# Attention steps placed by hand in a two-layer graph transformer kernel, its pairs of tiles, its query bias and the PSUM places of its border queries

## The chip, the core and the metric

The kernel runs on one core of a Trainium2 chip. The metric is device time in microseconds (us) for one execution; the time given for the kernel before is the median of its runs. Five engines work side by side, each on its own instructions in order: PE (matrix multiplication), DVE (vector work), ACT (activations, scaling and copies), POOL (here above all the indirect transfers, called gathers) and SP (which only issues transfers). An instruction waits until what it needs is there, and everything behind it on the same engine waits with it. 16 DMA engines move data between the core's memory and HBM.

## The reference

2708 nodes with 512 features pass through two equal layers of a graph transformer: attention with 8 heads of 64 over the neighbours in an adjacency matrix, then a feed-forward network with 2048 hidden units, each with a residual and a normalization.

```
mask = adj + eye
q, k, v = (h @ Wq.T + bq), (h @ Wk.T + bk), (h @ Wv.T + bv)      # 8 heads of 64
scores = where(mask == 0, -1e9, q . k / 8)
ctx = softmax(scores) @ v
h1 = layer_norm(h + ctx @ Wo.T + bo)
h2 = layer_norm(h1 + relu(h1 @ W1.T + b1) @ W2.T + b2)
```

The matrix is sparse: a node has some 9 neighbours. All is in float32.

## The kernel before, in words

The function `by_edges` does the work; `by_rows` is a dense way for inputs that break the assumptions, and does not run here. The 2708 nodes are 22 tiles of up to 128 rows (the last, tile 21, has 20). The kernel first makes, for each node, the list of its neighbours, and then sorts the nodes by the length of their lists, so that tile 0 holds the nodes with the longest lists. `CAPS` (L37) is how many neighbours the tiles have at most: 22, 14, 13, ... 5, 3.

**Start (L859 to L999).** `first` runs over the tiles in their given order: PE makes keys k and values v of a tile (`project`, L570), DVE adds the key bias and ACT copies the values, and the rows go to HBM (`kv_d`). Beside that the adjacency rows come in (`aj`, SP), ACT turns them into codes (L689), and DVE finds the neighbours by rounds of maxima (L692 to L699), 1.3 lists per tile. k waits for DVE in one of three PSUM places with the tag g, v for ACT in one of three with the tag f. The bias of the queries, `bq`, is needed as a row on all partitions: `turned_row` (L556) makes a diagonal matrix `dg` on DVE, multiplies it on PE with ones into `pr`, and copies that on DVE. Before, this happens after the seventh tile (QT, L921), while the key bias is turned at the first. `first_queries` then makes the queries of all tiles, the order of the nodes (`ranked`, `inverted`), and the first attention steps.

**Attention (L1087 to L1171, L1513).** Tiles follow in the order of `blocks` (L1508), pairs of tiles, 11 of them. A tile is cut into chunks of two neighbours per node (`SLOTS`). One attention step takes one chunk: POOL gathers two rows of keys and values per node (L1061, three chunks ahead), DVE multiplies the keys with the query and sums per head into the scores `sc` (L1098, L1104), ACT takes the exponentials `p` (L1117) and weights half of the values (L1124), DVE weights the other half and adds up (L1130, L1137). The second part of a chunk is written one step behind its first. After a tile's last chunk DVE makes the sums, and ACT divides into `cx` (L1168). At most three tiles may be ready at a time (`CXB`); then no further step is made. `attend` is a generator, and each of its steps costs as much credit as the chunk is wide (a full chunk 1). `advance(more)` (L1570) adds credit and makes steps while there is some; `through(k)` makes all steps up to the end of pair k.

**A block of the main loop (L1650 to L1719).** For each pair of tiles, `feed_forward` (L1384) runs 16 steps f: PE multiplies W1 with the turned tile into `pf` (L1431, three PSUM places with the tag f), ACT evicts it into `ft` (L1442), and PE multiplies the `ft` of three steps before with W2 into `a` (L1404). After the last step DVE adds the residual and normalizes both tiles (`norm`, L1215: statistics, the inverse root on POOL as `rd`, two passes). Between these steps the main loop puts in: the keys and values for the next layer of the block before (`behind`, layer 0, f = 5 to 8), the context of the next pair, turned at f = 10 (`attended`, L1351, with `cT`), its projection `o` and normalization at f = 11 (in block 0 of layer 0 at f = 12 and 13), and attention steps by `advance`. The numbers in `PACE` (L50) are the credit per step f, for f up to 2, 3 to 10 and from 11; inside the normalizations at f = 11, `advance(0.5)` follows each tile. The order in which the engines' instructions stand is just the order in which this loop writes them.

**Border (L1625 to L1646).** Layer 1's queries need the end of layer 0. 20 of them are made in a row, with attention steps (`advance(0.55)`) between, before its first block; DVE scales and adds the bias (`qs`, L1337), and SP writes them to `q_d`. All these queries use the PSUM places g.

Of the kernel before, what the change touches and what calls it, by code (L numbers as in the profile page):

```python
# [46 lines left out]
OWN = 7  # L47
LISTS = (6, 9, 11, 14, 15, 17, 18, 19, 20, 21)
EARLY = 3
PACE = ((0.45, 0.8, 0.55), (0.5, 0.8, 0.7))  # L50


@with_exitstack
# [419 lines left out]
def by_edges(ctx: ExitStack, tc: tile.TileContext, x, xT, adj, layers, out, redo):  # L473
# [385 lines left out]
    def first(w, meanwhile):  # L859
# [32 lines left out]
        finish(halves)  # L892
        turning = turned_row(cols[0], "bk", 1.0)
        bk = next(turning)
        wv = matrix(w, "Wv", "wv")
        pa = tc.tile_pool(name="pa", bufs=2)
        lists, counted, placing = lists_of(pa.__enter__())
        done, before = 0, None
        for t in range(NT):
            r = size(t)  # L900
            if t == NT - 1:
                counts = counted()
            xs = tokens(t, 0)
            kv = wts.tile([P, 2 * DM], F32, tag=f"w2_{5 + t % 3}", name="kvs")
            k = project(xs, r, wk, "k")
            if t == 0:
                finish(turning)
            if t < NT - 1:
                nc.vector.tensor_tensor(kv[:r, :DM], k[:r], bk[:r], ALU.add)
            v = project(xs, r, wv, "v", other=True)  # L910
            nc.scalar.copy(kv[:r, DM:], v[:r])
            if before:
                nc.scalar.dma_start(**before)
            before = dict(out=kv_d[0][t * P : t * P + r, :], in_=kv[:r])
            if t == 0:
                finish(load())
            while done < min(NT, 1 + LEAD * t):
                lists(done)
                done += 1
            meanwhile(t)  # L920
            if t == QT:  # L921
                wq = matrix(w, "Wq", "wq", nc.gpsimd)
                turning = turned_row(cols[1], "bq", DK**-0.5)
                bq = next(turning)
                finish(turning)

        def last_keys():
            nc.vector.tensor_tensor(kv[:r, :DM], k[:r], bk[:r], ALU.add)
# [314 lines left out]
    class Layer:  # L1243
        def __init__(self, n, w):
            self.n, self.w, self.w1, self.w2, self.due = n, w, [], [], None

        def load_first(self):
            w = self.w
# [83 lines left out]
        def query(self, g, zT):  # L1332

            r = size(g)
            q = project(lambda c: zT[:, c, :r], r, self.wq, "q")
            qs = dn.tile([P, DM], F32, tag="row", name="qs", bufs=3)
            nc.vector.scalar_tensor_tensor(  # L1337
                qs[:r], q[:r], DK**-0.5, self.bq[:r], ALU.mult, ALU.add
            )
            plus_rest(qs[:r], q, r, DK**-0.5)  # L1340
            self.kept()
            self.due = (g, qs)
# [162 lines left out]
    now = Layer(0, layers[0])  # L1505


    blocks = [(20, 19), (18, 17), (7, 9), (6, 10), (5, 11), (0, 16)]  # L1508
    blocks += [(1, 15), (2, 14), (3, 13), (4, 12), (NT - 1, 8)]
    NB = len(blocks)  # L1510
    order = [g for block in blocks for g in block]

    def attend(n, got):  # L1513
# [15 lines left out]
        for k, step in enumerate(steps):  # L1529
            if step:  # L1530
                g, s0, c, i, last = step
                if i == 0:
                    while q is None:
                        q = asked(n, g)
                        if q is None:
                            yield None
                    t, q = Tile(g, q), None
                if k > 0:
                    kv = next(loaded)
                t.weights(kv, s0, c)  # L1540
                if i > 0 and q is None and g != order[-1]:
                    q = asked(n, order[order.index(g) + 1])
                done.append((t, kv, s0, c, last))
            else:
                done.append(None)
# [43 lines left out]
    def beside_keys(t):  # L1589

        if t == NT - 5:
            now.load_first()
        if t > NT - 3:
            now.load_second(t + 2 - NT, temp)
            now.load_w1(t + 2 - NT, nc.gpsimd)
            now.load_w2(t + 2 - NT, nc.gpsimd)

    def beside_queries(t):

        if t < 2:  # L1600
            now.load_w1(t + 2, nc.gpsimd)
            now.load_w2(t + 2, nc.gpsimd)
        if t == 6:
            now.settle()
            now.load_w1(4, nc.scalar)
# [16 lines left out]
    for n in range(NL):  # L1622
        last = n == NL - 1
        nxt = None if last else Layer(n + 1, layers[n + 1])
        if n > 0:  # L1625
# [5 lines left out]
            next(ahead)  # L1631
            next(streamed)
            while pool:
                advance(0.55)
                now.query(*pool.pop(0))
            for _ in streamed:
                advance(0.55)
            through(0)
            early[n] = now.attended(blocks[0], got)
            next(early[n])  # L1640
# [2 lines left out]
            for _ in blocks[0]:  # L1643
                next(early[n])
            finish(streamed)
            now.load_w2(NFC // 2 - 1)  # L1646
        *_, hs = early[n]
        hT = now.turned(blocks[0], hs)
        turning = projecting = None
        for k, block in enumerate(blocks):  # L1650
# [4 lines left out]
            for f, zs in enumerate(now.feed_forward(block, hs, hT)):  # L1655
# [6 lines left out]
                    projecting = now.attended(blocks[k + 1], got)  # L1662
                    next(projecting)
                if more and f == 11 + 2 * (k + n == 0):
                    for hs_next in projecting:
                        advance(0.5 if k else 0.0)
                advance(PACE[n][(f > 2) + (f > 10)] if k else 0.8 if f < 11 else 0.4)
                if f in (0, 3, 7, 9):
                    next(asking, None)
                if more and f == NFC - 1:  # L1670
# [11 lines left out]
                if not more and f == 0:  # L1682
                    finish(ahead)
                if not last:
                    if (k, f) == (0, 15):
                        now.load_next()
                    if (k, f) == (0, 12):
                        now.kv = [matrix(nxt.w, "Wk", "wk", nc.scalar)]
# [4 lines left out]
                    if (k, f) == (NB - 1, 0):  # L1693
                        places.clear()
                        now.wq = matrix(nxt.w, "Wq", "wq")
                    if f == 1 and k in (1, 3):
                        i, name, scale = (1, "bk", 1.0) if k == 1 else (0, "bq", DK**-0.5)
                        turning = turned_row(now.cols[i], name, scale)
                        rows_of = now if k == 1 else nxt
                        setattr(rows_of, name, next(turning))  # L1700
                    if f == 3 and k in (1, 3):
                        finish(turning)
                if not last and not more:
                    if f % 2:
# [81 lines left out]
```

## Time and profile before

| | us |
|---|---|
| median of 3 runs | 2006.22 (2001.13 to 2008.62) |
| the profiled execution | 2005.24 |
| its span, first to last instruction | 2003.5 |
| PE busy in it | 1872.3 (93%) |
| DVE busy | 1388.8 (69%) |
| ACT busy | 935.0 (47%) |
| POOL busy | 753.9 (38%) |

The profile is one execution. A row of its timeline gives the start in us from the beginning of the span, the duration, the engine, the line of the kernel, the operation, what it writes and reads, and in brackets how long the engine had been idle and what ended that. A row of its groups has, behind the bar, the busy time, the mean duration in ns, and the idle time before. A row of its stretches gives the length, the busy time of the engines with the number of instructions in brackets, the granted clock of PE, and the share and rate of DMA. A row of waits gives the sum, the number and the longest.

### The profile page before, as it was taken

What the parts mean: (1) busy time and instruction counts of PE and PEld (TensorE: products, weight loads), DVE (VectorE), ACT (ScalarE), POOL (GpSimd) and SP (SyncE); (2) the same over time, 40 slices, a digit from 0 to 9 for tenths busy, and PEclk for the clock granted to TensorE, in tenths of its full rate; (3) what the DMA queues carried; (4) which work ended last, traced back from release to release, by engine and by line L of the source; (5) the groups of instructions that cost most, each with busy time, mean ns of one, the idle gap of its engine ahead of it and who ended that gap; (6) DMA issues with size and microseconds to landing.
All of it is one profiled execution on the core that took longest, in us unless ns stands there. A gap on an engine that the chain in (4) does not pass through costs nothing. (4 is left out here: it accounts for less than half of the span.)

```text
span 2003.5 us, 20880 instructions
## 1 busy us (share of the span) xinstructions
PE 1872.3 (93%) x6172; PEld 1102.0 (55%) x6172; DVE 1388.8 (69%) x2181; ACT 935.0 (47%) x3218; POOL 753.9 (38%) x721
## 2 busy tenths in 40 slices
PE   8699979999899999897999998998999998998997
PEld 4244446665556555564655633665655655565664
DVE  5797779787877877857142156789999999765413
ACT  4451346555555555634221213556655665553311
POOL 2102655454544545433001042344564655432102
PEclk9899989999999999998999999999999999999999
DMA  8798958556545466533101676836665665532000
GB/s 317 265 338 282 347 187 298 175 187 204 204 167 198 164 214 231 168 129 98 53 20 50 225 260 228 266 135 219 214 220 196 222 251 177 179 107 96 16 1 19
DMA packets 131355, 366.91 MB, mean 183 GB/s; under 512 B 19290, under 2 KB 37546, under 8 KB 128524
## 3 DMA queue, kind: packets, MB, share of 16 engines
q0 software_dynamic: 70608, 252.12, 36.6%
q1 hardware_dynamic: 50580, 95.47, 13.9%
q10 hardware_dynamic: 10044, 17.91, 2.5%
q8 instruction: 50, 0.82, 0.2%
q14 instruction: 73, 0.60, 0.1%
HBM read 314.79 MB, written 50.65 MB: 182 GB/s over the span
## 5 line engine op out<-in xcount | busy, mean ns | idle before, releaser
L1431 PE MATMUL pf<-hT,w 128*128 128x256 f32 (+1 forms) x2816 | 645.0, 377 | 50.6 <-ACT ft L1442 42.4
L1404 PE MATMUL a<-w,ft 128*128 128x512 f32 x1312 | 628.4, 605 | 29.2 <-ACT ft L1442 29.2
L1431 PEld LDWEIGHTS pf<-hT,w 128*128 128x128 f32 x2816 | 523.5, 193 | 231.7 <-issue 103.2
L1061 POOL DMA_INDIRECT kv<-kv_d,listed x420 | 506.5, 1206 | 234.5 <-issue 107.3
L1404 PEld LDWEIGHTS a<-w,ft 128*128 128x128 f32 x1312 | 251.8, 195 | 231.1 <-issue 169.1
L1224 POOL TENSOR_TENSOR rd<-va,mhalf 128x1 f32<-128x1 f32 (+1 forms) x88 | 81.9, 931 | 638.9 <-DVE va L1222 638.9
L1124 ACT ACTIVATE kv<-kv,p 128x64 f32<-128x64 f32 x1232 | 311.0, 335 | 5.0
L1442 ACT ACTIVATE ft<-pf,b 128x256 f32<-128x256 f32 (+1 forms) x336 | 151.0, 459 | 292.5 <-PE pf L1431 292.4
L1098 DVE TENSOR_TENSOR kv<-kv,q 128x1024 f32<-128x1024 f32 (+3 forms) x222 | 256.6, 1156 | 19.3 <-DMA q<-q_d,ident_i 12.8
L1117 ACT ACTIVATE p<-sc,listed 128x8 f32<-128x8 f32 x420 | 104.9, 298 | 352.8 <-DVE sc L1104 346.4
L1104 DVE TENSOR_REDUCE sc<-kv 128x16 f32<-128x1024 f32 (+3 forms) x222 | 257.9, 1162 | 7.6
L1137 DVE TENSOR_TENSOR acc<-acc,kv 128x1024 f32<-128x1024 f32 (+2 forms) x178 | 205.2, 1153 | 42.1 <-ACT kv L1124 26.4
L1130 DVE TENSOR_TENSOR kv<-kv,p 128x512 f32<-128x512 f32 (+1 forms) x178 | 122.7, 689 | 97.0 <-ACT p L1117 97.0
L580 PE MATMUL o<-wo,cT 128*128 128x512 f32 x336 | 150.6, 601 | 5.1 <-ACT cT L1239 5.1
L580 PEld LDWEIGHTS o<-wo,cT 128*128 128x128 f32 x336 | 64.5, 193 | 87.5 <-issue 71.6
L1488 DVE TENSOR_TENSOR kvs<-k,bk 128x512 f32<-128x512 f32 (+1 forms) x22 | 15.2, 689 | 130.2 <-PE k L580 128.9
L1168 ACT ACTIVATE cx<-acc,su 128x64 f32<-128x64 f32 (+1 forms) x352 | 88.2, 333 | 35.9 <-DVE flags L1554 21.1
L692 DVE MAX8 tops<-code 128x8 f32<-128x247 f32 (+2 forms) x242 | 78.6, 399 | 22.6 <-ACT code L689 22.4
L1228 DVE SCALAR_TENSOR_TENSOR h<-h,rd,ln_b 128x512 f32<-128x512 f32 (+1 forms) x88 | 66.1, 751 | 39.9 <-POOL rd L1224 39.9
L689 ACT ACTIVATE code<-aj 128x2708 bf16<-128x2708 int32 (+1 forms) x22 | 73.0, 3324 | 42.8 <-POOL aj L685 42.8
L1124 ACT ACTIVATE acc<-kv,p 128x64 f32<-128x64 f32 (+1 forms) x352 | 88.8, 335 | 1.4
L1024 POOL DMA_INDIRECT kv_d<-kvs,ident_i x22 | 24.7, 1124 | 166.0 <-ACT kvs L1491 123.6
(169 smaller groups left out, 1576.7 us busy)
## 6 DMA issues: line engine op xcount, KB each, us to landing
aj<-in_adj SPq DMA_DIRECT2D x21, 1354.0 KB, 8.7
kv_d<-kvs ACTq DMA_DIRECT2D x21, 512.0 KB, 7.6
xg<-in_xT SPq DMA_DIRECT2D x19, 512.0 KB, 7.8
w<-in_W SPq DMA_DIRECT2D x16, 512.0 KB, 6.4
kv<-kv_d,listed POOLq DMA_INDIRECT x420, 6.0
q_d<-qs SPq DMA_DIRECT2D x22, 256.0 KB, 5.7
zT_d<-zT SPq DMA_DIRECT2D x22, 256.0 KB, 3.8
xb_d<-h SPq DMA_DIRECT2D x21, 256.0 KB, 6.5
```

Of the source, the lines that this page charges most:

```text
L580: nc.tensor.matmul(o[:r], xs(c), wm[:, c, :], start=(c == 0), stop=(c == NC - 1))
L1061: return nc.gpsimd.indirect_dma_start(out=to, out_offset=None, in_=table[:, :], in_offset=bass.IndirectOffsetOnAxis(ap=s, axis=0), bounds_ ...
L1098: nc.vector.tensor_tensor(kv[:r, :c, :DM], kv[:r, :c, :DM], self.q[:r].unsqueeze(1).to_broadcast([r, c, DM]), ALU.mult,)
L1104: nc.vector.tensor_reduce(self.sc[:r, s0 : s0 + c, :], kv[:r, :c, :DM].rearrange("p s (h d) -> p s h d", d=DK), AX.X, ALU.add,)
L1117: nc.scalar.activation(p[:r, s, :], self.sc[:r, s, :], AF.Exp, bias=minus[:r, g, s : s + 1])
L1124: nc.scalar.activation(to[:, i, hd], kv[:r, i, DM + h * DK : DM + (h + 1) * DK], AF.Copy, scale=p[:r, s0 + i, h : h + 1],)
L1130: nc.vector.tensor_tensor(to[:, 0, :].rearrange("p (h d) -> p h d", d=DK), kv[:r, 0, DM:].rearrange("p (h d) -> p h d", d=DK), p[:r, s0, : ...
L1137: nc.vector.tensor_tensor(self.acc[:r, :c, :], self.acc[:r, :c, :], kv[:r, :c, DM:], ALU.add)
L1168: nc.scalar.activation(cx[:r, hd], self.acc[:r, 0, hd], AF.Copy, scale=self.su[:r, h : h + 1])
L1404: nc.tensor.matmul(a[:r], fts[f][:, c0 : c0 + r], self.w2[f // 2][:, f % 2, :], start=(f == 0), stop=(f == NFC - 1),)
L1431: nc.tensor.matmul(pf[:, :w], self.w1[f // 2][:, c, f % 2 * P : f % 2 * P + P], hT[:, c, :w], start=(c == 0), stop=(c == NC - 1),)
L1442: nc.scalar.activation(ft[:, :w], pf[:, :w], AF.Relu, bias=self.b1[:, f : f + 1])
```

## The change

Eight edits, all in `by_edges`:

1. The credit per step f comes from two tables of 16 numbers per layer, `PACES` for block 0 and `PACE` for the others. There is none for f = 0 and 1 and for f = 11 and 12 (in block 0 of layer 0: f = 0 to 3, 12 and 13; in that of layer 1: 11 and 12). `advance` between the two normalizations at f = 11 is gone.
2. The pairs of tiles from the third on are others: by neighbours, before 11, 14, 19, 20, 20, 29, 22, 21, 20, 21, 13 (the sums of `CAPS`), now 11, 14, 19, 19, 20, 20, 20, 20, 21, 21, 25. The longest tile, 0, is now in the last pair, with the small tile.
3. The query bias of layer 0 is turned at the start, with the key bias.
4. The queries of the border use the PSUM places g and f in turn.
5. At the border, steps are made only until two tiles are ready, at 0.6 for 0.55.
6. The query of the next tile is fetched from the first chunk of a tile on, not from the second.
7. The first weight loads go through SP's and ACT's queues in place of POOL's.
8. The biases for layer 1 are turned between f = 0 and 4, not 1 and 3, of blocks 1 and 3, and their columns are loaded at f = 9 of block 0, not 15.

```diff
+PACES = (
+    (0.0,) * 4 + (0.85,) * 8 + (0.0,) * 2 + (0.8,) * 2,
...
-PACE = ((0.45, 0.8, 0.55), (0.5, 0.8, 0.7))
+PACE = (
+    (0.0,) * 2 + (0.6,) * 3 + (1.2,) * 4 + (0.6,) * 2 + (0.0,) * 2 + (0.8,) * 3,
+    (0.0,) * 2 + (0.82,) * 9 + (0.0,) * 2 + (1.0,) * 3,
+)
...
         turning = turned_row(cols[0], "bk", 1.0)
         bk = next(turning)
+        turning_q = turned_row(cols[1], "bq", DK**-0.5)
+        bq = next(turning_q)
...
                 finish(turning)
+                finish(turning_q)
...
                 wq = matrix(w, "Wq", "wq", nc.gpsimd)
-                turning = turned_row(cols[1], "bq", DK**-0.5)
-                bq = next(turning)
-                finish(turning)
...
+            self.apart, self.other = True, False
...
-            q = project(lambda c: zT[:, c, :r], r, self.wq, "q")
+            self.other = not self.other
+            q = project(lambda c: zT[:, c, :r], r, self.wq, "q", self.other and self.apart)
...
-    blocks = [(20, 19), (18, 17), (7, 9), (6, 10), (5, 11), (0, 16)]
-    blocks += [(1, 15), (2, 14), (3, 13), (4, 12), (NT - 1, 8)]
+    blocks = [(20, 19), (18, 17), (8, 9), (7, 10), (6, 11), (5, 12)]
+    blocks += [(4, 13), (3, 14), (2, 15), (1, 16), (NT - 1, 0)]
...
-                if i > 0 and q is None and g != order[-1]:
+                if q is None and g != order[-1]:
...
-            now.load_w1(t + 2 - NT, nc.gpsimd)
-            now.load_w2(t + 2 - NT, nc.gpsimd)
+            now.load_w1(t + 2 - NT, nc.gpsimd if t == NT - 2 else nc.sync)
+            now.load_w2(t + 2 - NT)
...
-            now.load_w1(t + 2, nc.gpsimd)
-            now.load_w2(t + 2, nc.gpsimd)
+            now.load_w1(t + 2, nc.scalar)
+            now.load_w2(t + 2, nc.scalar)
...
-                advance(0.55)
+                advance(0.6)
                 now.query(*pool.pop(0))
             for _ in streamed:
-                advance(0.55)
+                if len(got) < 2:
+                    advance(0.6)
...
+            now.apart = False
...
-                    for hs_next in projecting:
-                        advance(0.5 if k else 0.0)
-                advance(PACE[n][(f > 2) + (f > 10)] if k else 0.8 if f < 11 else 0.4)
+                    *_, hs_next = projecting
+                advance((PACE if k else PACES)[n][f])
...
-                    if (k, f) == (0, 15):
+                    if (k, f) == (0, 9):
...
-                    if f == 1 and k in (1, 3):
+                    if f == 0 and k in (1, 3):
...
-                    if f == 3 and k in (1, 3):
+                    if f == 4 and k in (1, 3):
```

What the tables move is seen in the order of the instructions. On DVE, in block 5 of layer 1 before, the normalizations of the next pair at f = 11 stand like this (`h` is the tile, `o` its projection, `kv` a chunk, `sc` its scores):

```order
L1366 TENSOR_TENSOR h<-o,xb 128x512
L1218 BN_STATS st<-h 128x6
L1220 BN_AGGR mv<-st 128x2
L1222 TENSOR_SCALAR va<-mv 128x1
L1225 SCALAR_TENSOR_TENSOR h<-h,mv,ln_g 128x512
L1228 SCALAR_TENSOR_TENSOR h<-h,rd,ln_b 128x512
L1098 TENSOR_TENSOR kv<-kv,q 128x2x512
L1104 TENSOR_REDUCE sc<-kv 128x16
L1130 TENSOR_TENSOR kv<-kv,p 128x512
L1137 TENSOR_TENSOR acc<-acc,kv 128x1024
L1366 TENSOR_TENSOR h<-o,xb 128x512
L1218 BN_STATS st<-h 128x6
```

On DVE in the same block of the changed kernel (its lines are 7 to 10 higher):

```order
L1375 TENSOR_TENSOR h<-o,xb 128x512
L1225 BN_STATS st<-h 128x6
L1227 BN_AGGR mv<-st 128x2
L1229 TENSOR_SCALAR va<-mv 128x1
L1232 SCALAR_TENSOR_TENSOR h<-h,mv,ln_g 128x512
L1235 SCALAR_TENSOR_TENSOR h<-h,rd,ln_b 128x512
L1375 TENSOR_TENSOR h<-o,xb 128x512
L1225 BN_STATS st<-h 128x6
L1227 BN_AGGR mv<-st 128x2
L1229 TENSOR_SCALAR va<-mv 128x1
L1232 SCALAR_TENSOR_TENSOR h<-h,mv,ln_g 128x512
L1235 SCALAR_TENSOR_TENSOR h<-h,rd,ln_b 128x512
```

The attention step between the two normalizations has moved to f = 13. On ACT at the same place before, from the eviction of f = 11 to that of f = 12 (`ft`; `p` are exponentials of a chunk, `kv` and `acc` its weighted values, `cx` the divided context):

```order
L1442 ACTIVATE ft<-pf,b_7375 128x256
L1117 ACTIVATE p<-sc,listed 128x8 x2
L1124 ACTIVATE kv<-kv,p 128x64 x8
L1117 ACTIVATE p<-sc,listed 128x8 x2
L1124 ACTIVATE acc<-kv,p 128x64 x8
L1117 ACTIVATE p<-sc,listed 128x8 x2
L1124 ACTIVATE kv<-kv,p 128x64 x8
L1168 ACTIVATE cx<-acc,su 128x64 x8
L1442 ACTIVATE ft<-pf,b_7375 128x256 x2
```

On ACT of the changed kernel, the contexts of the next pair turned (`cT`) and what follows:

```order
L1246 ACTIVATE cT<-tp,bv 128x128 x8
L1124 ACTIVATE p<-sc,listed 128x8 x2
L1131 ACTIVATE kv<-kv,p 128x64 x8
L1451 ACTIVATE ft<-pf,b_7375 128x256 x3
L1124 ACTIVATE p<-sc,listed 128x8 x2
L1131 ACTIVATE acc<-kv,p 128x64 x8
L1451 ACTIVATE ft<-pf,b_7375 128x256
```

Between the evictions of f = 11, 12 and 13 no attention stands any more. On PE before, at the seventh tile of the start, the turning of the query bias (`pr`) stands between a value and a key projection:

```order
L580 MATMUL k<-wk,xg 128x512 x4
L580 MATMUL v<-wv,xg 128x512 x4
L567 MATMUL pr<-dg,ones 128x128 x4
L580 MATMUL k<-wk,xg 128x512 x4
L580 MATMUL v<-wv,xg 128x512 x4
```

On PE of the changed kernel, at its beginning:

```order
L587 MATMUL k<-wk,xg 128x512 x4
L574 MATMUL pr<-dg,ones 128x128 x8
L587 MATMUL v<-wv,xg 128x512 x4
L587 MATMUL k<-wk,xg 128x512 x4
L587 MATMUL v<-wv,xg 128x512 x4
```

Both biases are now turned behind the first key projection, and the later place is gone.

More of the change, by code (lines that the diff above doesn't have):

```diff
@@ L49 @@
 EARLY = 3
-PACE = ((0.45, 0.8, 0.55), (0.5, 0.8, 0.7))
+PACES = (
+    (0.0,) * 4 + (0.85,) * 8 + (0.0,) * 2 + (0.8,) * 2,
+    (0.75,) * 11 + (0.0,) * 2 + (0.9,) * 3,
+)
+PACE = (
+    (0.0,) * 2 + (0.6,) * 3 + (1.2,) * 4 + (0.6,) * 2 + (0.0,) * 2 + (0.8,) * 3,
+    (0.0,) * 2 + (0.82,) * 9 + (0.0,) * 2 + (1.0,) * 3,
+)
 @with_exitstack
```

## Prediction

> **What bounds the kernel now.** I read the table of stretches first, with its cuts at the stages: the start (keys, values, lists, first queries), block 0 of layer 0, its blocks 1 to 8, block 9, the border (block 10 and the queries of layer 1), block 0 of layer 1, its blocks 1 to 8, block 9, the end. Then the waits of PE, then the timeline inside the largest of them.
>
> ```profile
> core 0: us, PE busy (x) PEld busy (x) DVE busy (x) ACT busy (x) POOL busy (x), PEclk, DMA share, GB/s
> 0.00:275.70 275.70, 249.96 (x643) 112.81 (x643) 206.09 (x572) 114.17 (x159) 84.33 (x126) 0.97 0.84 294
> 275.70:351.20 75.50, 65.95 (x225) 42.27 (x226) 61.83 (x82) 41.90 (x161) 43.97 (x38) 0.93 0.79 276
> 351.20:1030.90 679.70, 642.12 (x2129) 390.31 (x2128) 483.61 (x648) 344.85 (x1291) 284.05 (x244) 0.98 0.48 162
> 1030.90:1107.10 76.20, 76.20 (x265) 46.22 (x264) 17.20 (x32) 14.56 (x42) 7.80 (x9) 1.00 0.13 46
> 1107.10:1262.90 155.80, 141.75 (x466) 69.83 (x464) 73.02 (x109) 37.82 (x137) 39.15 (x38) 0.97 0.73 252
> 1262.90:1331.30 68.40, 68.40 (x241) 42.82 (x242) 53.27 (x71) 38.02 (x143) 22.21 (x19) 1.00 0.56 186
> 1331.30:1894.50 563.20, 529.16 (x1793) 335.11 (x1792) 466.23 (x616) 326.34 (x1239) 256.61 (x216) 0.97 0.50 174
> 1894.50:1956.10 61.60, 61.60 (x226) 39.32 (x225) 14.45 (x28) 11.22 (x32) 5.78 (x7) 1.00 0.02 9
> 1956.10:2003.50 47.40, 37.18 (x195) 23.29 (x193) 13.12 (x31) 6.15 (x16) 10.03 (x30) 0.93 0.06 20
> sum 2003.50, PE 1872.31 PEld 1101.98 DVE 1388.81 ACT 935.03 POOL 753.92; mean PE 208.03 PEld 122.44 DVE 154.31 ACT 103.89 POOL 83.77
> ```
>
> PE is the bound: it is busy 1872.3 of 2003.5 us. Where no attention is left (the two ninth blocks) it is never idle, at clock 1.00. Those two blocks give the clean price: 76.2 us with keys and values of the block before, 61.6 us without. Each projects the 20-row tile for the next block; a full tile costs more by
>
> ```profile
> L580 PE MATMUL o<-wo,cT 128*128 128x512 f32 x336 | 150.6, 601 | 5.1 <-ACT cT L1239 5.1
> ```
>
> 150.6 / 42 = 3.6 us, of which I take 2.6 as the difference (estimate: the four quarters of the small tile run side by side). So a clean block is 78.8 us in layer 0 and 64.2 us in layer 1. Against that, blocks 1 to 8 of layer 0 lose 679.7 - 8 x 78.8 = 49 us (37.6 of it idle), those of layer 1 lose 563.2 - 8 x 64.2 = 50 us (34.0 idle), block 0 of layer 0 loses 75.5 - 64.2 = 11 us. The border has 14.1 us idle. Who ends PE's waits:
>
> ```profile
> PE pf L1431 <- ACT ft L1442: 42.4, 12, 9.2
> PE a L1404 <- ACT ft L1442: 29.2, 15, 4.6
> PE pr L567 <- DVE dg L561: 22.2, 3, 17.9
> PE o L580 <- ACT cT L1239: 5.1, 1, 5.1
> PE q L580 <- DVE qs L1337: 4.0, 2, 3.2
> ```
>
> It is mostly the eviction ft on ACT, a 0.5 us instruction that comes late. Why, the timeline of block 5 in layer 1 shows (starts in us, then durations):
>
> ```profile
> 1655.29 0.69 DVE L1366 TENSOR_TENSOR h<-o,xb 128x512 f32<-128x512 f32 x1
> 1658.23 0.75 DVE L1228 SCALAR_TENSOR_TENSOR h<-h,rd,ln_b 128x512 f32<-128x512 f32 x1 [0.46 <-POOL rd L1224]
> 1661.41 0.49 ACT L1117 ACTIVATE p<-sc,listed 128x8 f32<-128x8 f32 x2 [4.70 <-DVE sc L1104]
> 1669.33 0.49 ACT L1117 ACTIVATE p<-sc,listed 128x8 f32<-128x8 f32 x2 [5.37 <-DVE sc L1104]
> 1673.68 0.81 ACT L1442 ACTIVATE ft<-pf,b 128x256 f32<-128x256 f32 x2
> 1674.19 3.78 PE L1431 MATMUL pf<-hT,w 128*128 128x256 f32 x8 [5.17 <-ACT ft L1442]
> ```
>
> DVE normalizes one tile (1655.29 to 1658.98: 3.7 us), then an attention step, then the other tile. ACT has the exponentials of that step ahead of ft and idles twice, 4.70 and 5.37 us, for the scores that stand behind the normalization; ft comes at 1673.68 and PE has stood 5.17 us. PE then runs eight pf matmuls in 3.78 us, which is part of why the loss exceeds the idle time.
>
> **Part by part.** *Query bias turned first.* At the seventh tile PE waits for dg, which stands on DVE behind the lists:
>
> ```profile
> 74.84 2.07 PE L567 MATMUL pr<-dg,ones 128*128 128x128 f32 x8 [17.93 <-DVE dg L561]
> 76.95 0.69 DVE L568 COPY bq<-pr 128x512 f32<-128x512 f32 x1 [1.58 <-PE pr L567]
> 81.30 0.69 DVE L909 TENSOR_TENSOR kvs<-k,bk 128x512 f32<-128x512 f32 x1 [3.66 <-PE k L580]
> 88.61 3.58 DVE L692 MAX8 tops<-code 128x8 f32<-128x247 f32 x11 [6.62 <-ACT code L689]
> 60.00:75.00 15.00, 0.16 (x1) 0.16 (x1) 14.26 (x53) 6.99 (x3) 4.16 (x10) 0.55 0.98 384
> 75.00:90.00 15.00, 15.00 (x37) 7.62 (x38) 3.14 (x9) 5.27 (x3) 0.45 (x1) 0.88 0.34 112
> ```
>
> PE loses 17.9 us and about 2 in the slow stretch behind it: 20 at most. But DVE, with the lists, then paces PE, because k waits in three PSUM places for DVE; DVE itself loses 1.58 + 3.66 + 6.62 = 11.9 us through that wait. That is the lower value if the lists rule to their end. DMA allows it: its share falls to 0.34 for 15 us just there, so there are about 9 us of transfer time to fill in. I take 14, between 11.9 and 20, nearer to DVE's figure; 8 if the transfers, at 0.98 before, don't keep up. The four added dg and the copy at the very start cost nothing that I can see: DVE has no list to work on yet. The weight loads that leave POOL's queue for SP's and ACT's pass nothing that is late: I count 0.
>
> *Block 0 of layer 0, no step for f below 4.* The loss there is one wait:
>
> ```profile
> 288.32 1.23 DVE L1098 TENSOR_TENSOR kv<-kv,q 128x1024 f32<-128x1024 f32 x1 [8.35 <-DMA q<-q_d,ident_i]
> 293.80 3.60 PE L1431 MATMUL pf<-hT,w 128*128 128x256 f32 x8 [9.25 <-ACT ft L1442]
> ```
>
> DVE waits 8.35 us for a query row that can only be fetched when all are written, ACT waits for DVE, ft for ACT. With the steps held back, ft has nothing ahead of it. 11 us goes to 2: gain 9; 5 if the query is still late at f = 4. The earlier request for the next tile's query helps here and is counted with it.
>
> *Steps away from the normalizations, balanced pairs.* Now DVE's budget. A chunk of two rows costs it
>
> ```profile
> L1098 DVE TENSOR_TENSOR kv<-kv,q 128x1024 f32<-128x1024 f32 (+3 forms) x222 | 256.6, 1156 | 19.3 <-DMA q<-q_d,ident_i 12.8
> L1104 DVE TENSOR_REDUCE sc<-kv 128x16 f32<-128x1024 f32 (+3 forms) x222 | 257.9, 1162 | 7.6
> L1137 DVE TENSOR_TENSOR acc<-acc,kv 128x1024 f32<-128x1024 f32 (+2 forms) x178 | 205.2, 1153 | 42.1 <-ACT kv L1124 26.4
> L1130 DVE TENSOR_TENSOR kv<-kv,p 128x512 f32<-128x512 f32 (+1 forms) x178 | 122.7, 689 | 97.0 <-ACT p L1117 97.0
> L1061 POOL DMA_INDIRECT kv<-kv_d,listed x420 | 506.5, 1206 | 234.5 <-issue 107.3
> ```
>
> 1.156 + 1.162 + 1.153 + 0.689 = 4.2 us. Before, blocks with DVE at 466 of 563 us were followed by two with nearly none. Over the ten blocks of layer 1 DVE's work is 53.3 + 466.2 + 14.5 = 534 us, 53 per block, against 64.2 of PE. The new tables give layer 1 10.4 chunks a block (0.82 x 9 + 3), the pairs hold 9.5 to 10.5, so the load is even and the demand just met. In a step of f, PE takes about 3.4 us (1.7 for pf, 1.7 for a, from (64.2 - 3.6 x 2 - 2) / 16) and DVE 0.82 x 4.2 = 3.4: level. In layer 0 the four steps at 1.2 want 20 us of DVE, but f = 6 and 7 also hold keys and values on PE, 7.2 us each, so there are 28. In f = 11, where the projection o makes the step 10.6 us long, DVE has the two normalizations alone, 7.4 us and an addition each. POOL's gathers, two per chunk at 1.2 us, hide under that: 2.4 of 3.4 us. What is left I put at 2 us a block in place of 6: the clean price is unlikely with DVE near 0.85 busy. Layer 1: 50 - 16 = 34; layer 0: 49 - 18 = 31 (this holds the two waits for dg at 0.8 and 3.5 us, which turning at f = 0 and 4 should end). Ends: 15 each if half the waits only move; 44 and 42 at the clean price.
>
> One rule weighs on the remainder. Of waits of different length the clock shows
>
> ```profile
> 400.00:450.00 50.00, 47.38 (x166) 29.85 (x165) 44.35 (x65) 26.10 (x100) 27.30 (x23) 1.00 0.55 186
> 1650.00:1700.00 50.00, 44.83 (x145) 27.93 (x144) 46.17 (x61) 30.63 (x119) 24.95 (x21) 0.93 0.50 162
> ```
>
> the stretch that holds 2.6 us of idle time keeps clock 1.00, the one with the 5.17 us wait has 0.93. So short waits cost their own length, and I add nothing for the clock to the 2 us. The Trainium skill (TensorE: Matmul & The Clock Gate, Part 1) says the clock halves after an idle window of about 3.4 us that runs freely; by that rule, too, waits of 2 us cost nothing more. If instead every wait cost clock in proportion, as 16 of 50 us in layer 1 are not idle, the remainder would be 3 us a block and the sum 16 us worse.
>
> *What gets worse.* In block 0 of layer 1 fewer attention steps are made ahead; three chunks must follow at once at f = 10, before PE can turn the context of tile 17. That is 3 x 4.2 us on DVE and about 3 on ACT, 16 us, of which PE covers a part: -12 (0 to -16) where that block now has no wait. The ninth blocks carry attention now: -2 each.
>
> *Border.* In the waits o for cT, 5.1, and q for qs, 4.0:
>
> ```profile
> 1234.75 0.49 ACT L1117 ACTIVATE p<-sc,listed 128x8 f32<-128x8 f32 x2 [4.04 <-DVE sc L1104]
> ```
>
> ACT holds a step of the next block's attention, which waits 4.04 us for DVE, ahead of cT. The new condition (no steps once both tiles are there) takes that away; twice the PSUM places let PE run ahead of the evictions of qs, at most 4.0 us. Gain 9 with what the clock gives back, 0 if the attention of block 0 itself ends no sooner.
>
> *Sum.* 14 + 9 + 34 + 31 + 9 - 12 - 4 = 81 us. The profiled execution took 2005.24 us for its span of 2003.5; it becomes 1924. The median of the three runs, 2006.22, lies 1 us above the profiled one: 1925.
>
> **The rivals.** *Half of it (the waits move).* If DVE, at 0.85 busy, falls behind the tables, ft is late elsewhere, at f = 5 to 8 of layer 0 and at f = 9 and 10 of layer 1, and the start is held by the transfers. For it: 4.8 chunks in four steps, and a DVE that runs level with PE leaves no reserve. Against it: the longer steps at f = 6 and 7. It gives 8 + 5 + 15 + 15 + 5 - 12 - 4 = 32 us: 1974, and with part of it anything from 1951 up.
>
> *No change (the change doesn't do what it says).* If ft is late because DVE has too much work and not because of where the steps stand, the 65 us of the blocks stay: 14 + 9 + 9 - 12 - 4 = 16 us at best, less where the start gives 8 and the border nothing: 1 us. About 2000 to 2005. Against it: layer 0, with DVE at 484 of 680 us, loses as much as layer 1 at 466 of 563; a plain lack of DVE time would show in layer 1 alone.
>
> *Slower (the attention becomes the bound).* The place is the transposes of the context at f = 10: PE waits for cx, and nothing can be put ahead of it. Five of sixteen steps of f have no attention now; DVE's normalizations fill 7.4 us at the block's start and 7.4 in the middle. If DVE idles for the remainder of these stretches, 5 x 3.4 + 7.2 - 15 = 9 us, it has 64.2 - 9 = 55 for work of 53: it fits. Each microsecond lacking per block costs 10 us over layer 1. The sign turns at a lack of 8 us; 10 us lacking give 1925 + 100 = 2025. For it: in the blocks before, the attention was two blocks ahead at the end, a reserve that is gone. Against it: the row of L1098 above has 19.3 us idle in all 222 chunks, so key rows are hardly ever late.
>
> **How the numbers follow.** Forecast, gains of 55 to 125 us: 0.64. Better than that: 0.03. Half of it: 0.18. No change: 0.08. Slower: 0.07. The measurement tells about 0.5%, 10 us, from no change. So faster is 0.64 + 0.03 + 0.18 = 0.85, the same 0.08, slower 0.07. The range starts at 1882: the upper ends 20 + 11 + 44 + 42 + 12 make 129 with nothing lost, 1877, and they will hardly all come at once. It ends at 1972, which takes in most of the half case and leaves out no change and slower, 0.15, and a few hundredths more.
>
> **What would show it.** In the profile after: the wait of pr for dg (17.9) is gone and the list stage ends 12 to 20 us sooner; pf's and a's waits for ft fall from 71.6 us to about 30; ACT has no wait of 4 us or more for sc between the normalizations; blocks 1 to 8 take about 81 us in layer 0 and 66 in layer 1, with DVE even over ten blocks; a wait of tp for cx stands in block 0 of layer 1. The forecast is wrong if the blocks keep 84 and 70 us while the waits for ft only change their f, or if PE waits for cT in every block.

## The result and the profile after

The changed kernel takes 1900.22 us (median of 4 runs, 1895.18 to 1901.63); the kernel before, on the same chip, 2005.35 us. The ratio is 0.9472, with a 95% interval of 0.9447 to 0.9498. It is 105 us faster where 81 were forecast.

The profiled execution took 1895.18 us, its span 1893.4. This is the table of stretches of the kernel after, cut at the same nine stages as the one of before:

```profile
core 0: us, PE busy (x) PEld busy (x) DVE busy (x) ACT busy (x) POOL busy (x), PEclk, DMA share, GB/s
0.00:267.10 267.10, 252.66 (x642) 112.57 (x642) 206.52 (x572) 114.03 (x159) 77.59 (x119) 0.99 0.88 303
267.10:336.50 69.40, 65.10 (x224) 41.04 (x224) 48.97 (x64) 34.59 (x131) 38.82 (x34) 1.00 0.78 263
336.50:965.80 629.30, 628.72 (x2128) 386.49 (x2129) 471.86 (x635) 334.37 (x1254) 277.48 (x243) 1.00 0.52 175
965.80:1042.00 76.20, 76.20 (x265) 46.23 (x264) 42.86 (x63) 30.03 (x110) 13.72 (x13) 1.00 0.22 74
1042.00:1189.80 147.80, 139.23 (x465) 69.14 (x463) 65.71 (x101) 32.82 (x117) 35.37 (x35) 0.98 0.71 248
1189.80:1265.20 75.40, 70.75 (x240) 43.89 (x241) 63.87 (x85) 45.14 (x173) 26.09 (x22) 0.98 0.59 210
1265.20:1776.70 511.50, 510.02 (x1794) 329.36 (x1793) 445.14 (x585) 312.44 (x1181) 259.19 (x214) 1.00 0.56 191
1776.70:1838.30 61.60, 61.60 (x226) 39.33 (x225) 32.65 (x52) 22.57 (x80) 6.96 (x7) 1.00 0.03 9
1838.30:1893.40 55.10, 37.16 (x195) 23.27 (x193) 13.09 (x31) 6.14 (x16) 9.71 (x30) 0.89 0.05 17
sum 1893.40, PE 1841.44 PEld 1091.31 DVE 1390.65 ACT 932.12 POOL 744.93; mean PE 204.60 PEld 121.26 DVE 154.52 ACT 103.57 POOL 82.77
```

Row by row against before: the start is 8.6 us shorter, block 0 of layer 0 6.1, its blocks 1 to 8 50.4, block 9 0, the border 8.0; block 0 of layer 1 is 7.0 longer, its blocks 1 to 8 51.7 shorter, block 9 0, the end 7.7 longer. Together 110.1 us; the profiled execution is the fastest of the four, so the rows give some 5 us more than the medians. The sixteen inner blocks carry 102 of them, and there PE is idle for only 0.6 and 1.5 us. DVE's work is the same (1390.7 us, before 1388.8), but the ninth blocks now hold 42.9 and 32.7 us of it instead of 17.2 and 14.5, and take exactly as long as before. PE's own busy time falls too, from 1872.3 to 1841.4 us, with the granted clock at 0.992 over the span for 0.975.

PE's waits in the kernel after (sum, times, longest):

```profile
PE k L587 <- DVE kvs L919: 7.0, 3, 3.9
PE q L587 <- DMA zT<-zT_d: 7.0, 1, 7.0
PE k L587 <- DMA wk<-in_Wk: 5.0, 1, 5.0
PE tp L1241 <- ACT cx L1175: 4.7, 3, 4.4
PE pf L1440 <- ACT hT L1246: 4.6, 5, 1.5
PE tp L1241 <- DVE h L1235: 3.4, 2, 2.9
PE pf L1440 <- ACT ft L1451: 0.8, 1, 0.8
```

The waits for ft, 71.6 us in the kernel before, are down to 0.8. What is left stands in the start, at the end of block 0 of layer 0 (h), at the border, in block 0 of layer 1 and at the beginning of some blocks (hT). ACT's wait for scores in layer 1's blocks shows the same; first before, then after:

```profile
ACT p L1117 <- DVE sc L1104: 134.1, 60, 9.0
```
```profile
ACT p L1124 <- DVE sc L1111: 18.9, 22, 2.9
```

This is the timeline of the kernel after around the normalizations of f = 11, in a block of layer 1 (start, duration, engine):

```profile
1558.88 7.03 PE L587 MATMUL o<-wo,cT 128*128 128x512 f32 x16
1559.70 0.45 ACT L1451 ACTIVATE ft<-pf,b 128x256 f32<-128x256 f32 x1
1562.51 0.69 DVE L1375 TENSOR_TENSOR h<-o,xb 128x512 f32<-128x512 f32 x1 [0.83 <-PE o L587]
1565.74 1.89 PE L1440 MATMUL pf<-hT,w 128*128 128x256 f32 x8
1566.12 0.68 DVE L1375 TENSOR_TENSOR h<-o,xb 128x512 f32<-128x512 f32 x1
1567.67 0.47 ACT L1451 ACTIVATE ft<-pf,b 128x256 f32<-128x256 f32 x1 [7.52 <-PE pf L1440]
1569.71 1.22 DVE L1105 TENSOR_TENSOR kv<-kv,q 128x1024 f32<-128x1024 f32 x1
```

DVE does one normalization after the other, and its next step begins only at 1569.71. ACT stands 7.52 us, but for PE and with nothing ahead of ft: ft comes 0.04 us after the end of the pf that it evicts (1565.74 + 1.89 = 1567.63). This wait of ACT for PE costs nothing; the waits of ACT for DVE, with ft behind them, did.

### The profile page after: what moved, and what is told of

It reads as the page before. It is cut to its first block, busy times and chain, and to the rows that moved or that the text cites. A ratio compares the mean times of both kernels' runs of the same rounds, so it can differ in the third digit from the quotient of the medians.

```text
span 1893.4 us, 20835 instructions
## 1 busy us (share of the span) xinstructions
PE 1841.4 (97%) x6172; PEld 1091.3 (58%) x6172; DVE 1390.7 (73%) x2181; ACT 932.1 (49%) x3218; POOL 744.9 (39%) x714
## 5 line engine op out<-in xcount | busy, mean ns | idle before, releaser
L1440 PE MATMUL pf<-hT,w 128*128 128x256 f32 (+1 forms) x2816 | 632.8, 372 | 6.2 <-ACT hT L1246 4.6
L1413 PE MATMUL a<-w,ft 128*128 128x512 f32 x1312 | 611.1, 592 | 0.0
L1413 PEld LDWEIGHTS a<-w,ft 128*128 128x128 f32 x1312 | 246.8, 190 | 187.4 <-issue 170.4
L1105 DVE TENSOR_TENSOR kv<-kv,q 128x1024 f32<-128x1024 f32 (+1 forms) x222 | 256.6, 1156 | 17.8 <-DMA q<-q_d,ident_i 11.5
L1111 DVE TENSOR_REDUCE sc<-kv 128x16 f32<-128x1024 f32 (+1 forms) x222 | 257.9, 1162 | 7.6
L587 PE MATMUL k<-wk,xg 128*128 128x512 f32 x168 | 82.4, 636 | 12.0 <-DVE kvs L919 7.0
L699 DVE MAX8 tops<-code 128x8 f32<-128x247 f32 (+2 forms) x242 | 78.7, 400 | 17.8 <-ACT code L696 17.6
L1375 DVE TENSOR_TENSOR h<-o,xb 128x512 f32<-128x512 f32 (+1 forms) x44 | 30.2, 686 | 83.6 <-PE o L587 32.6
```

The lines of the kernel that those rows point to most:

```text
L587: nc.tensor.matmul(o[:r], xs(c), wm[:, c, :], start=(c == 0), stop=(c == NC - 1))
L1105: nc.vector.tensor_tensor(kv[:r, :c, :DM], kv[:r, :c, :DM], self.q[:r].unsqueeze(1).to_broadcast([r, c, DM]), ALU.mult,)
L1111: nc.vector.tensor_reduce(self.sc[:r, s0 : s0 + c, :], kv[:r, :c, :DM].rearrange("p s (h d) -> p s h d", d=DK), AX.X, ALU.add,)
L1413: nc.tensor.matmul(a[:r], fts[f][:, c0 : c0 + r], self.w2[f // 2][:, f % 2, :], start=(f == 0), stop=(f == NFC - 1),)
L1440: nc.tensor.matmul(pf[:, :w], self.w1[f // 2][:, c, f % 2 * P : f % 2 * P + P], hT[:, c, :w], start=(c == 0), stop=(c == NC - 1),)
```

## The experiments

Where nothing else is said, a kernel is the changed one with a single edit, the one shown. Two theories stood against each other for the blocks: **place** (ft is late because a step's exponentials stand ahead of it while DVE normalizes) and **balance** (DVE had too much to do in some blocks). The kernel after took 1900.22 us. The runs were made in sets, each beside its own runs of the kernel before (2002.93 to 2005.38 us), to which the ratios refer; between sets, a few us of a time mean little.

**The old pairs, the new places.**

```diff
-    blocks = [(20, 19), (18, 17), (8, 9), (7, 10), (6, 11), (5, 12)]
-    blocks += [(4, 13), (3, 14), (2, 15), (1, 16), (NT - 1, 0)]
+    blocks = [(20, 19), (18, 17), (7, 9), (6, 10), (5, 11), (0, 16)]
+    blocks += [(1, 15), (2, 14), (3, 13), (4, 12), (NT - 1, 8)]
```

> The changed kernel with the pairs of tiles of before; the new tables of credit stay. Theory P (the blocks' 102 us came from where the steps stand): only the two blocks that must finish the pair of tiles 0 and 16 (29 rows) lose, because 9 and 7 rows are then forced at f = 10; they cost some 10 to 15 us each, so 1920 to 1930 us, and all other blocks stay within 1 us of 78.3 and 63.7 us. Theory B (the gain came from the even load): the load of before comes back with the pairs, half of the 102 us or more is lost, 1950 us or above.

1940.48 us, ratio 0.9686 (0.9665 to 0.9708). Between the two expectations. The waits of PE, and the largest in the timeline:

```profile
PE tp L1241 <- ACT cx L1175: 34.5, 9, 14.3
636.35 1.90 PE L1241 MATMUL tp<-ident,cx 128*128 128x128 f32 x4 [14.28 <-ACT cx L1175]
```

Blocks 1 to 8 take 656.8 us in layer 0 and 525.1 in layer 1, 61 less than before. Twelve of the sixteen run at the mean price of the kernel after, within 1 us. The other four hold a new wait; in the largest, the pair with 29 rows isn't ready at f = 10, its chunks follow at once and PE waits for the context. That block is 17.5 us longer and the one at the same place of layer 1 14.1; the other two, 5.6 and 3.9 us, neither expectation had. So the place carries the first 61 us and the even pairs the other 41.

**The new pairs, the old places.** The two tables and the main loop's `advance` as before:

```diff
-                    *_, hs_next = projecting
-                advance((PACE if k else PACES)[n][f])
+                    for hs_next in projecting:
+                        advance(0.5 if k else 0.0)
+                advance(PACE[n][(f > 2) + (f > 10)] if k else 0.8 if f < 11 else 0.4)
```

> The changed kernel with the credit per step of before, the step between the two normalizations included; the balanced pairs stay. Theory P: the blocks go back to about 84 and 70 us, and block 0 of layer 0 to 75; 80 to 105 us of the gain are lost, 1980 to 2005 us, with PE's waits for ft near 70 us. Theory B: the even pairs keep most, 1930 us or less.

2011.56 us, ratio 1.0037 (1.0024 to 1.005): all gain gone, and a little slower than before (the end of the span keeps its 7.6 us more). The largest waits of PE are again

```profile
PE pf L1433 <- ACT ft L1444: 59.8, 15, 9.3
PE a L1406 <- ACT ft L1444: 22.9, 8, 5.4
```

and blocks 1 to 8 take 679.8 us in layer 0 and 568.0 in layer 1, before 679.7 and 563.2. Even pairs without the places bring nothing. Uneven load was not the cause of the old waits, then; evening it out only removes a wait that the new places would meet.

**One step back between the two normalizations.** Of the places only this:

```diff
-                    *_, hs_next = projecting
+                    for hs_next in projecting:
+                        advance(0.5 if k else 0.0)
```

> The changed kernel with only one thing put back: an attention step after each of the two normalizations at f = 11 (credit 0.5 each); the new tables stay for all other f. If the step between the normalizations is what made ft late, each of the 16 inner blocks gets back a wait of 3 to 5 us: 1900 + 50 to 80 = 1950 to 1980 us, with ACT idle for sc of 4 to 5 us beside it. If the tables elsewhere did it, within 15 us of 1900.

1960.31 us, ratio 0.9783 (0.976 to 0.9806): 60 us. Blocks 1 to 8 of the two layers, and PE's waits:

```profile
339.30:1009.10 669.80, 639.81 (x2130) 388.63 (x2128) 479.74 (x641) 342.21 (x1279) 281.84 (x246) 0.98 0.50 167
1309.60:1840.00 530.40, 514.47 (x1793) 328.79 (x1791) 446.49 (x586) 314.60 (x1189) 258.02 (x214) 1.00 0.53 184
```
```profile
PE a L1413 <- ACT ft L1451: 27.0, 15, 5.1
PE pf L1440 <- ACT hT L1246: 20.4, 13, 3.8
```

DVE's work in layer 1 is that of the kernel after (446.5 and 445.1 us), and the stretch is 18.9 us longer; in layer 0 40.5. The line moves up to one credit per block to between the tiles. This is the place theory at its narrowest, and more than half of the blocks' gain. It doesn't hold for each block: the first two of layer 1 lose nothing. That a later normalization, and so a later hT, is part of the price was not forecast. With all places of before the blocks lose 107 us; the 48 us beyond the 59 here go with the other numbers of the tables, and which of them matter wasn't tried.

**Query bias at the seventh tile.** The three lines that turn it moved back.

```diff
-        turning_q = turned_row(cols[1], "bq", DK**-0.5)
-        bq = next(turning_q)
...
-                finish(turning_q)
...
+                turning = turned_row(cols[1], "bq", DK**-0.5)
+                bq = next(turning)
+                finish(turning)
```

> The changed kernel with the query bias turned at the seventh tile again. If the lists on DVE and the transfers pace the start, it loses what the stretch up to the first pf showed, 8 to 9 us: 1909 us. If PE's own wait were the price, it would lose the 18 to 20 us of that wait: 1919 us.

1904.53 us, ratio 0.9509 (0.9488 to 0.9531). Its start takes 273.3 us, after's 267.1:

```profile
0.00:273.30 273.30, 249.00 (x642) 112.35 (x642) 206.34 (x572) 114.24 (x159) 78.74 (x119) 0.97 0.85 297
60.00:75.00 15.00, 2.01 (x9) 2.02 (x10) 12.96 (x48) 5.47 (x3) 3.62 (x8) 0.50 0.93 364
```
```profile
60.00:75.00 15.00, 15.00 (x36) 6.65 (x35) 13.63 (x48) 8.31 (x5) 3.81 (x9) 1.00 0.97 363
75.00:90.00 15.00, 12.34 (x29) 5.17 (x28) 10.97 (x39) 9.34 (x5) 1.26 (x5) 0.98 1.00 360
88.25 5.40 PE L587 MATMUL k<-wk,xg 128*128 128x512 f32 x8 [2.67 <-DVE kvs L919]
```

The first two rows are of the experiment, the other three of the kernel after. PE's wait for dg (17.6 us) is back, and yet only about 6 us of span come with it, less than both expectations. Without it PE works through the 15 us from 60 on, but then waits for kvs instead, 7.0 us in all, and behind two of these waits eight matmuls take 5.40 us in place of 3.60. So the 20 us that PE could win are not there. kvs waits on DVE behind a list:

```profile
82.47 3.58 DVE L699 MAX8 tops<-code 128x8 f32<-128x247 f32 x11 [0.42 <-ACT code L696]
87.52 0.67 DVE L919 TENSOR_TENSOR kvs<-k,bk 128x512 f32<-128x512 f32 x1
```

The size of these 6 us is loose: in ten executions of different kernels with the bias first, the start took 266.0 to 271.3 us, and in three with the bias at the seventh tile 272.6 to 275.7.

**The border as before.** One set of PSUM places, the old steps.

```diff
-            self.apart, self.other = True, False
+            self.apart, self.other = False, False
...
-                advance(0.6)
+                advance(0.55)
...
-                if len(got) < 2:
-                    advance(0.6)
+                advance(0.55)
```

> The changed kernel with the border of before: queries in one set of PSUM places, steps made without end at 0.55. If these two edits brought the border's 8 us, 1908 us, with waits of q for qs and of o for cT of 4 to 5 us each again. If the wait of q for zT on SP's queue (7.0 us after, 2.7 before) only changes places with them, within 3 us of 1900.

1896.35 us, ratio 0.9475 (0.9448 to 0.9501): no difference. Two waits of PE that are back, then the border and block 0 of layer 1:

```profile
PE o L587 <- ACT cT L1246: 5.1, 1, 5.1
PE q L587 <- DVE qs L1346: 3.8, 1, 3.8
```
```profile
1042.90:1197.80 154.90, 142.27 (x466) 70.13 (x464) 73.05 (x109) 37.79 (x137) 38.06 (x38) 0.96 0.72 253
1197.80:1266.20 68.40, 68.40 (x240) 42.84 (x241) 53.27 (x71) 38.07 (x143) 22.15 (x19) 1.00 0.56 187
```

The wait of q for zT falls from 7.0 to 1.5 us beside it. The border is 7.1 us longer and block 0 7.0 shorter, which neither expectation had. The edits move the attention of block 0's tiles, and its wait, from one stage to the other. Going on with steps to the border's end while keeping the two sets of places

```diff
-            finish(streamed)
+            for _ in streamed:
+                advance(0.6)
```

> The changed kernel with attention steps (credit 0.6) beside the last four queries of the border, after the contexts of block 0 are turned. If block 0 of layer 1 loses its 7 us (wait of tp for cx 4.4 us) because too few steps were made ahead, that block falls from 75.4 to 68.4 us and the border stays near 148: 1893 us. If the steps delay the turning of h, the border grows by what the block gains: 1900 us.

gives 1898.51 us, ratio 0.9476 (0.9454 to 0.9498), the same again: block 0 takes 70.3 us and the border 153.2.

**The first weight loads back on POOL's queue.**

```diff
-            now.load_w1(t + 2 - NT, nc.gpsimd if t == NT - 2 else nc.sync)
-            now.load_w2(t + 2 - NT)
+            now.load_w1(t + 2 - NT, nc.gpsimd)
+            now.load_w2(t + 2 - NT, nc.gpsimd)
...
-            now.load_w1(t + 2, nc.scalar)
-            now.load_w2(t + 2, nc.scalar)
+            now.load_w1(t + 2, nc.gpsimd)
+            now.load_w2(t + 2, nc.gpsimd)
```

> The changed kernel with the first weight loads on POOL's queue again. The end of the program after the last output is 7.4 us longer in the changed kernel and in all four experiments so far. If POOL's queue leaves that behind because of the moved loads, it falls back to the 1.9 us of before: 1893 us. If something else lengthens it, 1900, the start as in the changed kernel.

1891.09 us, ratio 0.9439 (0.9416 to 0.9462). The end takes 47.5 us in place of 55.1; no other stage differs by more than 1.2 us. **The same loads taken off POOL's queue in the kernel before**, with nothing else changed (that diff with its - and + exchanged, on the kernel before):

> The kernel before with one edit of the change alone: the first W1 and W2 loads leave POOL's queue for SP's and ACT's. Theory A, that POOL's closing DRAIN grows with these loads off its queue whatever the rest of the kernel is: DRAIN 9.3 us in place of 1.9, and 2009 to 2013 against 2003 to 2006 for the kernel before, with the stages unchanged up to the last put. Rival B, that the DRAIN is a matter of the new order at the end (the attention of the last blocks): DRAIN stays at 1.9 us and the time within 2 us of the kernel before.

2011.48 us, ratio 1.003 (1.0018 to 1.0042), and the end of the span is 7.7 us longer. The two last stretches, of the loads on POOL's queue after and off it before:

```profile
1842.10:1889.60 47.50, 37.21 (x195) 23.30 (x193) 13.15 (x31) 6.15 (x16) 10.07 (x30) 0.95 0.06 20
```
```profile
1952.60:2007.70 55.10, 37.21 (x195) 23.30 (x193) 13.15 (x31) 6.14 (x16) 10.07 (x30) 0.87 0.05 17
```

All engines do the same work in both. What differs is the DRAIN that POOL's sequencer runs behind its last put: 1.867 us in the kernel before and here with the loads on POOL, 9.298 in the kernel after and here with them off it. The new order at the end has no part in it.

**The border's query rows written by ACT.**

```diff
-                nc.sync.dma_start(out=q_d[self.n][g * P : g * P + r, :], in_=qs[:r])
+                (nc.scalar if self.apart else nc.sync).dma_start(
+                    out=q_d[self.n][g * P : g * P + r, :], in_=qs[:r]
+                )
```

> The changed kernel with the border's writes of queries to HBM issued by ACT in place of SP. If zT comes late (wait of 7.0 us) because its load stands on SP behind writes that wait for DVE, the wait goes and the border falls from 148 to 141 us, unless the attention of its block 0 then ends it: 1893 to 1900 us, with a wait of tp or o for cx or cT in the latter case.

1892.39 us, ratio 0.9439 (0.9415 to 0.9462). The wait of q for zT, 7.0 us, is 0.9 in three parts. SP's queue of writes, which wait for qs, had held up the loads of zT. The border takes 144.8 us, 3.0 less and not the expected 7. Though the median is 7.8 us lower, more than these 3 us can't be put down to the edit: the span of the profiled execution is only 1.6 us shorter than that of the kernel after.

**Both together.**

> The kernel after, with the first W1 and W2 loads back on POOL's queue and the query rows of the border written by ACT instead of SP; nothing else changed. Theory A, that the two gains seen one by one come from different places (the closing DRAIN of POOL, 7.4 us; the wait of q for zT at the border, 7.0 us, of which 3 stayed in the time): they add up, 1900 - 9 - 8 = 1883 to 1886, with DRAIN at 1.9 us and no wait of q for zT over 1 us. Rival B, that both are one reserve (whatever frees SP's or POOL's queue gives the same 8 us): 1890 to 1892 again.

1887.52 us, ratio 0.9415 (0.9402 to 0.9428): above the expected sum and below the rival's figure. In the profile both are there (DRAIN 1.867, q for zT 0.2), so they are two places. Beside the loads on POOL alone (1891.09 us) the writes on ACT bring 3.6 us, and the border is 145.9 us for 148.9; what each is worth in the time is known only to about 3 us.

**And the table of block 0 of layer 1 at 1.0.**

```diff
-    (0.75,) * 11 + (0.0,) * 2 + (0.9,) * 3,
+    (1.0,) * 11 + (0.0,) * 2 + (0.9,) * 3,
```

> As the one before, and the table of block 0 of layer 1 at 1.0 instead of 0.75 for f = 0 to 10, so that no rows are left over for the turn of f = 10. Theory A, that the 7 us of that block are the chunks which had to follow at once: the wait of tp for cx (4.4 us) goes and the block falls from 75.4 to 68.5 to 71 us, the whole to 1876 to 1880. Rival B, that these chunks only move (the border has filled DVE, and the steps at 1.0 now delay the eviction ft): the block stays at 74 to 77 us with waits for ft or hT in place of the one for cx, the whole within 2 us of the kernel with the two changes alone.

1882.97 us, ratio 0.9383 (0.9369 to 0.9396), the fastest of all. The border, block 0, and PE's wait for the context:

```profile
1048.90:1192.30 143.40, 137.81 (x465) 69.06 (x463) 65.99 (x102) 32.58 (x117) 35.66 (x35) 1.00 0.75 263
1192.30:1265.40 73.10, 71.01 (x241) 44.18 (x242) 63.94 (x85) 44.92 (x173) 26.52 (x23) 0.98 0.60 202
```
```profile
PE tp L1241 <- ACT cx L1175: 1.9, 3, 1.6
```

Against the kernel before this edit (both together) the wait falls from 4.4 to 1.9 us and the block from 75.8 to 73.1, not to 71 or less. No wait for ft comes in its place, so the rival is out, but the expected size was too large: PE reaches the turn while ACT is still dividing into cx. The start was 4 us longer in this execution, with unchanged code there.

The earlier request for the next query (edit 6) and the biases turned at f = 0 and 4 (edit 8) were in every run of the changed kernel and were not tried alone. The waits for dg inside the blocks, 4.3 us before, are in none of these runs, also not with the old places, where the blocks are no shorter for it.

## Why the prediction was right, and where its sizes were off

The forecast was 1925 us, the result 1900; the mechanism held, and the sum of 81 us was 29 short of the 110 of the profiled executions. Part of that nearness is luck: the start, block 0 of layer 0, the border and the loads came out 17 us worse than forecast, the other terms 46 better. Term by term, in its order:

- **Start, +14:** measured 8.6, near the 8 that was given for the case that the transfers don't keep up. The step that failed is the choice between the ends. The lists end 10 us sooner, as their last row shows, before and after, and not the 12 to 20 that was to be the sign. Of the 20 us that PE could win, 7.0 went into new waits for kvs and 3.6 into slow matmuls behind them. DMA's share was 0.97 to 1.00 from 60 to 130 us; whether the transfers held the lists up wasn't separated:

```profile
164.42 0.24 DVE L696 MAX8 top<-cb 20x8 f32<-20x88 f32 x1
```
```profile
154.15 0.24 DVE L703 MAX8 top<-cb 20x8 f32<-20x88 f32 x1
```

- **Block 0 of layer 0, +9:** 6.1. PE's wait of 9.25 us for ft is down to 0.8; it now waits 2.9 us for h at the block's end. DVE's wait for the query row hasn't gone, it is longer than the 8.35 us of before:

```profile
282.97 1.23 DVE L1105 TENSOR_TENSOR kv<-kv,q 128x1024 f32<-128x1024 f32 x1 [11.54 <-DMA q<-q_d,ident_i]
```

So the query is still late at f = 4, for which the prediction gave 5. But the step stands later among the evictions: ACT idles 7.18 us for its scores in place of 12.49, and PE loses only the 0.8 us to it. With the old places, and the earlier request for the query still in, PE waits 9.3 us for ft again and the block takes 75.9 us. The held-back steps brought the gain, not the request.
- **Blocks 1 to 8, +31 and +34:** 50.4 and 51.7. The clean prices, 78.8 and 64.2 us, were right within 0.5 (78.7 and 63.9 on average). The failed step is the remainder of 2 us a block, put there because DVE and PE ran level at 3.4 us a step: it is nothing. The upper ends of 44 and 42 us, given for the clean price, were too low as well: against that price the prediction's own rows show losses of 50 and 49 us. In this row of layer 1, one of the fullest blocks, DVE is busy for 0.92 of the time and PE is never idle:

```profile
1521.80:1585.50 63.70, 63.70 (x225) 41.18 (x224) 58.48 (x76) 41.22 (x158) 35.25 (x29) 1.00 0.62 211
```

Level load costs PE nothing here. DVE feeds PE in the block only at the turn of f = 10 and at the normalizations; ft passes through ACT alone, and it may be late, as pf has three places. How late, the block before the change shows whose wait the prediction read. This is the pf whose ft came at 1673.68:

```profile
1658.53 1.89 PE L1431 MATMUL pf<-hT,w 128*128 128x256 f32 x8
```

It ended at 1660.42, so ft was 13.3 us late, and PE stood for 5.17 of these: some 8 us were free. What must not come is a longer delay in one piece, which the step between the normalizations was.
- **Ninth blocks, -4:** 0, for the same reason.
- **Border, +9, and block 0 of layer 1, -12:** 8.0 and -7.0. Each sign was right, and the wait of tp for cx stands where it was put:

```profile
1146.57 19.58 PE L587 MATMUL q<-wq,zT 128*128 128x512 f32 x40 [6.97 <-DMA zT<-zT_d]
1232.28 1.91 PE L1241 MATMUL tp<-ident,cx 128*128 128x128 f32 x4 [4.40 <-ACT cx L1175]
```

But the prediction summed a gain and a loss from separate places. They are one: the border edits only moved 7 us, as the run with the border of before shows. Of the wait for zT on SP's queue it had nothing.
- **The weight loads, 0:** -7.7, the one term that was missed outright: it was put at nothing. The prediction looked at what the loads pass on the new queues, not at what is left behind on the old one. The last put ends at 1999.14 us in the kernel before, 4.4 before the end of the span; in the kernel after, with a span of 1893.4:

```profile
1880.26 1.04 POOL L1031 DMA_INDIRECT out<-h,ident_i  x1 [1.08 <-DVE h L1235]
```

it ends at 1881.30, 12.1 before the end.

The rivals: half of it fell, as the old waits went and no new ones of any size came in the inner blocks. No change fell with the new pairs in the old places. Slower, through the turn at f = 10, is a real mechanism: with the old pairs it takes 34.5 us. With the even pairs PE waits for the context (cx) for more than 0.3 us in block 0 of layer 1 alone.

## What to carry to other kernels

Before counting how busy a second engine is, look for the one place where its work stands ahead of an eviction that the bound engine needs, with a long dependent chain in between: moving the step away from there was worth 60 us, at equal work. Evening out the load pays only after that, where a due time can be missed. And an edit that shifts transfers from one queue to another should be looked at to the last instruction of the queue that loses them.

## What the runs showed of the hardware

- POOL's closing DRAIN takes 9.298 us in all kernels here whose first weight loads are off POOL's queue, and 1.867 in all where they are on it, though POOL issues its gathers for 1800 us in both. Why these loads shorten it wasn't tried.
- Short waits can cost clock, but the length alone doesn't decide it. The prediction let waits of 2.6 us (2.33 and 0.29 in its row) cost only their own length. In the start of the kernel after, eight k take 3.60 us with no wait ahead and 5.40 behind a wait of 2.67 (the row of 88.25 us above), and PEclk is 0.93 in the 20 us from 90 on; in the fastest kernel they take 3.70 behind a wait of 1.99 and 5.40 behind one of 4.85. With the writes on ACT they take 3.70 behind a longer wait, and PEclk is 1.00 from 140 to 150 us there:

```profile
144.14 3.70 PE L587 MATMUL k<-wk,xg 128*128 128x512 f32 x8 [2.94 <-DVE kvs L919]
```

The Trainium skill (TensorE: Matmul & The Clock Gate, Part 1) puts the slow clock behind an idle window of about 3.4 us; here it stood already behind 2.67, and the measurement decides. So between 2.67 and 2.94 us these runs show both.
